# Layers of local attention: outputs by features, scores and outputs in one group each

## The chip, the cores and the metric

The kernel runs on one core of a Trainium2 chip. A core has five engines that run their own instruction queues in order and wait for one another through semaphores: TensorE (PE in the profile, with its weight loads as PEld), VectorE (DVE), ScalarE (ACT), GpSimd (POOL) and SyncE (SP, which here only issues DMAs). TensorE writes its results to PSUM; all other data of the kernel lies in SBUF. The metric is the device time of one launch in microseconds, the median of several runs.

## The reference

`x` holds 2 x 1024 tokens of 128 numbers. The network adds eight stages to it, one after the other. Six of them are small. Two are large and alike (`_L1_ffn_ref`, before and after the stage `L1_attn_b`): six layers, each made of local attention with 16 heads of 64 and a feed-forward block. Shortened:

```python
for i in range(6):
    x = attn_layer(shift_tokens(x), Wqkv[i], q_scale[i], k_scale[i], Wo[i]) + x
    x = ffn_layer(shift_tokens(x), ...) + x

def attn_layer(x, Wqkv, qs, ksc, Wo):        # x: b, 1024, 128
    q, k, v = split(x @ Wqkv)                # 16 heads of 64 each
    q, k = l2norm(q) * qs, l2norm(k) * ksc   # per head
    q, k = rotary(q), rotary(k)
    # windows of 32 queries see the 32 keys before them and their own 32
    attn = softmax(q . k * 8, masked)        # 32 x 64 per window and head
    return (attn @ v) @ Wo
```

`shift_tokens` takes the second half of the features from the token before. The feed-forward block is a layernorm, two products of 341 columns (one through an exact GELU), their product, and a product back to 128.

## The kernel before

The class `Layers` computes one such pass of six layers. Its unit is a tile of 128 tokens, `m`, numbered over layers, batches and tiles (`place`): 6 x 2 x 8 = 96 tiles per pass, 192 in both. All is in fp32. A tile takes these stages, named as methods:

- `project` (L1448): q and k, each in two halves of the rotary pair, four matmuls of 128 x 512 into PSUM banks of the pool `pj`. `squares` (L1457, ScalarE) writes the squares of a bank to SBUF, `rotate` (L1477, VectorE, two multiplications per bank) multiplies the same bank with rotary tables. The two engines read one PSUM bank one after the other, in the order in which the program names them.
- `halves`, `join`, `scale` (L1483, L1494, L1509, GpSimd): the sum of the halves' squares, the sum of the rotated parts, and the multiplication with the inverse length, which `lengths` (VectorE) and `inverses` (ScalarE: Relu, Ln, Exp) make.
- `flip` and `heads`: q and k transposed on TensorE (through the helper `to_psum`, whose transposes have line L201) and copied to SBUF by ScalarE.
- `project_v`, `values`, `windows`: v, copied to SBUF, and cut by DMAs on SP into `vw`, which holds for every window its 64 rows of v.
- `scores`: eight masks and 64 small matmuls per tile, in two parts of 32. A fp32 matmul is two instructions in the profile, each with its weight load.
- `below_max`, `exps`, `sums`: the softmax without its division; `sums` also makes the reciprocals `inv`.
- `flip_p`, `probabilities`: the exponentials transposed, so that keys lie on partitions, and copied to SBUF.
- `outputs` (L1647): 64 small matmuls in two parts. A block of transposed probabilities (64 keys x 32 queries) is loaded into the array and v (64 keys x 64 features) streams; the result has queries on partitions. `divide` (L1655, VectorE) multiplies with `inv` from PSUM to SBUF; `flip_o` transposes the result on TensorE (8 transposes); `features` (L1672, ScalarE) copies it to `outT`, with features on partitions.
- `project_out`, `add_out`: the product with `Wo`, and the addition to x.
- The feed-forward block works on four tiles at once (`ffn_...`, `gate...`, `value...`), so in one turn of four.

`turns` writes the order of all work by hand. The text `ORDER` lists stage names with arguments and a number: in turn n, the stage works on tile n minus that number, so a larger number is later and a negative one earlier. Each turn walks through the whole list, and every engine takes its instructions in that order; nothing is rescheduled. The numbers run from -3 to 11. `features` and `project_out` of a tile thus run two turns after its scores, and its `ffn_add` up to eleven turns after.

PSUM has eight banks: four in `pj` (projections, v, outputs, `y` and everything of the feed-forward block, handed out in turn), two for transposes (`tp`), two for scores. A piece of work that wants a bank waits for the last reader of the one that was handed out four (or two) before.

ScalarE's functions come in table sets. `gate` ends with an explicit load of the set that has Ln and Exp, when its three parts are done; the GELU's set is loaded when the first part runs. A load is inserted wherever a function is not in the set that is active.

## Time and profile before

| what | before |
|---|---|
| runs, us | 3993.75 median, 3986.62 to 4009.88 (3 runs) |
| span of the profiled execution, us | 3987.0 |
| TensorE busy | 3825.6 us, 96% |
| VectorE busy | 3116.1 us, 78% |
| GpSimd busy | 2535.5 us, 64% |
| ScalarE busy | 2414.0 us, 61% |
| granted TensorE clock, mean | 0.970 |

The profiled execution is one run; of its time the profile has the span from its first to its last instruction. Busy time is what the records of an engine cover; a matmul's record is longer than the time it keeps TensorE from the next (they are pipelined), so costs on TensorE are better read from the starts of successive work. A group line has the source line, the engine, the operation, tiles written and read, shapes, the count, the busy time of the group, the mean duration of one in ns, and the idle time before it with what ended it. A wait line names the waiting engine and line, what it waited for, and then the sum in us, the number of times and the longest. A windows line has, after the window's bounds and length, the busy us of each engine with instruction counts, the granted clock of TensorE, and the DMA engines' share. A timeline line has the start in us, the duration of the run of like instructions in us, and their count.

### The profile page before, as it was taken

How to read it: one execution, taken by the hardware profiler on the slowest of the kernel's cores; microseconds unless marked ns; L12 is line 12 of the kernel's file. 1: busy time of each engine (PE TensorE's matmuls, PEld its weight loads, DVE VectorE, ACT ScalarE, POOL GpSimd, SP SyncE). 2: the span in 40 equal slices, each digit the busy share in tenths (PEclk: the TensorE clock that was granted, in tenths of full speed). 3: DMA queues.
4: the chain of work that ended last, by engine and by line, in shares of the span. 5: the costliest groups of instructions: out<-in, count | busy, mean ns of one | idle time of the engine just before them, and what ended most of it. 6: DMA issues, size and time to landing. Idle time of an engine off the chain costs nothing.

```text
span 3987.0 us, 156275 instructions
## 1 busy us (share of the span) xinstructions
PE 3825.6 (96%) x67372; PEld 2521.5 (63%) x67372; DVE 3116.1 (78%) x6012; ACT 2414.0 (61%) x4582; POOL 2535.5 (64%) x1638
## 2 busy tenths in 40 slices
PE   7898979999999999999999779999999999999998
PEld 5646436666666666666666446666666666666665
DVE  7775877778787878787887667887878787878786
ACT  3444437766666666666666458666666666666665
POOL 4541448776766667767675467766767767666662
PEclk8899979999999999999999779999999999999999
DMA  3030313232333333323222033333333323332222
GB/s 87 2 85 8 79 62 75 67 92 69 78 84 75 78 78 73 88 72 77 63 70 67 9 95 70 75 85 75 86 71 73 92 68 77 85 76 67 66 68 54
DMA packets 217397, 281.11 MB, mean 71 GB/s; under 512 B 52493, under 2 KB 108682, under 8 KB 216586
## 3 DMA queue, kind: packets, MB, share of 16 engines
q1 hardware_dynamic: 216714, 271.12, 27.9%
q8 instruction: 536, 8.78, 1.0%
q14 instruction: 147, 1.20, 0.1%
HBM read 69.46 MB, written 3.28 MB: 18 GB/s over the span
## 4 chain that ended last, share of the span: by engine, by line
PE 87%; DVE 6%; DMA 2%; POOL 2%; ACT 1%; issue 1%; SPq 0%; DVEq 0%; POOLq 0%; ACTq 0%
PE pj_l L1448 17%; PE y_l L1679 9%; PE pv_l L1550 9%; PE tqk_l L201 9%; PE av_l L1647 8%; PE sc_l L1597 7%; PE tpr_l L201 4%; PE to_l L201 4%; PE fg_l L1753 3%; PE fy_l L1789 3%; PE fa_l L1774 3%; PE sc_l L1588 2%; DMA f0share_e<-f0d_e 1%; PE f0S_e L1239 1%; DVE t_l L1477 1%
## 5 line engine op out<-in xcount | busy, mean ns | idle before, releaser
L1477 DVE TENSOR_TENSOR t_l<-pj_l,rot_l 128x512 f32<-128x512 f32 x1536 | 968.1, 684 | 368.6 <-ACT sq_l L1457 356.6
L1494 POOL TENSOR_TENSOR raw_l<-t_l,t_l 128x1024 f32<-128x1024 f32 x384 | 907.8, 2364 | 532.5 <-DVE on_l L1655 285.0
L1448 PE MATMUL pj_l<-wqkv_l,x_l 128*128 128x512 f32 x1536 | 785.9, 614 | 6.5 <-DVE t_l L1477 4.2
L1509 POOL TENSOR_TENSOR raw_l<-raw_l,rn_l 128x1024 f32<-128x1024 f32 x384 | 723.2, 1902 | 94.6 <-ACT rn_l L1504 87.4
L1483 POOL TENSOR_TENSOR sq_l<-sq_l 128x512 f32<-128x512 f32 x384 | 490.8, 1278 | 311.8 <-ACT sq_l L1457 308.7
L1457 ACT ACTIVATE sq_l<-pj_l 128x512 f32<-128x512 f32 x768 | 461.5, 603 | 369.6 <-PE pj_l L1448 367.6
L201 PE MATMUL tqk_l<-ident_sb,raw_l 128*128 128x128 f32 x3072 | 452.7, 278 | 15.5 <-POOL raw_l L1509 13.9
L1527 ACT COPY qT_l<-tqk_l 128x512 f32<-128x512 f32 x384 | 224.8, 585 | 387.9 <-PE tqk_l L201 387.8
L201 PEld LDWEIGHTS tqk_l<-ident_sb,raw_l 128*128 128x128 f32 x3072 | 356.4, 142 | 160.7 <-issue 121.3
L1550 PE MATMUL pv_l<-wqkv_l,x_l 128*128 128x512 f32 x768 | 416.4, 624 | 6.1 <-DVE ln_xn_fl L1733 5.3
L1679 PE MATMUL y_l<-outT_l,wo_l 128*128 128x128 f32 x3072 | 393.7, 281 | 0.0
L1597 PEld LDWEIGHTS sc_l<-kT_l,qT_l 64*32 64x32 f32 x24576 | 295.4, 105 | 155.5 <-issue 145.1
L1679 PEld LDWEIGHTS y_l<-outT_l,wo_l 128*128 128x128 f32 x3072 | 357.5, 191 | 18.3 <-issue 1.0
L1448 PEld LDWEIGHTS pj_l<-wqkv_l,x_l 128*128 128x128 f32 x1536 | 256.3, 192 | 172.1 <-issue 111.2
L1647 PE MATMUL av_l<-vw_l,pT_l 64*32 64x64 f32 x24576 | 360.5, 224 | 2.1 <-issue 1.7
L1559 ACT COPY v_l<-pv_l 128x512 f32<-128x512 f32 x384 | 225.1, 586 | 225.4 <-PE pv_l L1550 205.5
L1655 DVE TENSOR_TENSOR on_l<-av_l,inv_l 128x512 f32<-128x512 f32 x384 | 247.4, 686 | 121.5 <-PE av_l L1647 121.3
L1647 PEld LDWEIGHTS av_l<-vw_l,pT_l 64*32 64x32 f32 x24576 | 294.2, 105 | 70.0 <-issue 63.6
L1597 PE MATMUL sc_l<-kT_l,qT_l 64*32 64x64 f32 x24576 | 329.8, 223 | 0.3 <-issue 0.3
L201 PEld LDWEIGHTS tpr_l<-ident_sb,pr_l 128*128 128x128 f32 x1536 | 189.1, 141 | 152.3 <-issue 116.8
L1607 DVE TENSOR_TENSOR pr_l<-sc_l,mx_l 128x512 f32<-128x512 f32 x384 | 265.6, 692 | 13.2
L201 PEld LDWEIGHTS to_l<-ident_sb,on_l 128*128 128x128 f32 x1536 | 183.2, 141 | 128.4 <-issue 110.9
(317 smaller groups left out, 6208.9 us busy)
## 6 DMA issues: line engine op xcount, KB each, us to landing
vw_l<-v_l SPq DMA_DIRECT2D x3024, 64.0 KB
wqkv_l<-in_Wqkv SPq DMA_DIRECT2D x36, 512.0 KB
f0share_e<-f0d_e SPq DMA_DIRECT2D x64, 256.0 KB
rot_l<-in_rotary SPq DMA_DIRECT2D x24, 512.0 KB
wo_l<-in_Wo SPq DMA_DIRECT2D x12, 512.0 KB
w_l<-in_W SPq DMA_DIRECT2D x12, 341.0 KB
a0rows<-a0both SPq DMA_DIRECT2D x4, 512.0 KB
a0qk<-a0rows SPq DMA_DIRECT2D x32, 64.0 KB
```

The costliest lines, as they stand in the source:

```text
L201: self.nc.tensor.transpose(tp[:, c, :], src(c), self.ident)
L1448: self.nc.tensor.matmul(pj.rearrange("p h d -> p (h d)"), self.x[b][0][:, ts(a, P)], self.w[i]["qkv"][:, ds(INNER * s + 512 * u, 512)], st ...
L1457: self.nc.scalar.activation(st["sq", s][:, u], st["pj", s, u], AF.Square)
L1477: self.nc.vector.tensor_tensor(to, st["pj", s, u], tabs[:, k, None, ts(w, LD // 2)].to_broadcast(half), ALU.mult)
L1483: self.nc.gpsimd.tensor_tensor(sq[:, 0], sq[:, 0], sq[:, 1], ALU.add)
L1494: self.nc.gpsimd.tensor_tensor(r.rearrange("p h u d -> p u h d"), st["t1", s], st["t2", s], ALU.add)
L1509: self.nc.gpsimd.tensor_tensor(r, r, st["rn"][:, ts(s, LH), None].to_broadcast([P, LH, LD]), ALU.mult)
L1550: self.nc.tensor.matmul(pj, self.x[b][0][:, ts(a, P)], self.w[i]["qkv"][:, ds(2 * INNER + 512 * r, 512)], start=True, stop=True,)
L1597: nc.tensor.matmul(sc[j][ts(c, 32), hp, :], st["q"][rows, hp, ts(c, 32)], st["k"][rows, hp, ds(32 * c, 64)], start=False, stop=(hp == 7),)
L1607: nc.vector.tensor_tensor(p, st["sc"][j], mx[:, :, None].to_broadcast([P, 8, 64]), ALU.subtract)
L1647: nc.tensor.matmul(av[r][ts(c, 32), q, j, :], st["pT", j][rows, q, ts(c, 32)], st["vw"][rows, c, ts(2 * q + j, LD)], start=True, stop=True,)
L1679: self.nc.tensor.matmul(y[:, 0:P], self.w[i]["o"][:, c, :], st["o"][:, c, :], start=(c == 0), stop=(c == 7))
```

## The change

1. `outputs` is turned over: v (64 keys x 64 features) is loaded into the array and the transposed probabilities (64 keys x 32 queries) stream, so that the result has features on partitions. Its 64 matmuls are one group.
2. `flip_o` is gone; `features` copies from the outputs' banks.
3. `divide` now works on the exponentials in SBUF, in place, before `flip_p`.
4. `scores` is one group.
5. `ORDER` is another one. The numbers run from -3 to 12: all projections are three turns early, outputs two turns late (one before), the parts of the GELU lie in three turns (9, 10 and 11; before all in 9), `ffn_add` is at 12. In one of the four projections the rotation is named before the squares, in the other three after; before, the squares came first in all four.

```diff
 ORDER = """
-    value_in1:11 halves0:-2 join0:-2 add_out:3 flip11:0 divide0:2 divide1:2 project_v0:0 ffn_flip:7
-    heads01:0 flip_p0:1 gate_in0:9 heads11:0 value_in0:11 lengths1:-1 value1:11 value_in2:10 values0:0
-    scores0:0 lengths0:-2 inverses:-1 project10:-2 ffn_back:8 flip_p1:1 ffn_stats:7 gate0:9 value0:11
-    ffn_out:11 ffn_dev:7 squares10:-2 sums:1 ffn_norm:7 project11:-2 carry:0 project00:-3 value2:10
-    rotate10:-2 scores1:0 probabilities0:1 squares11:-2 project_v1:0 ffn_gain:8 probabilities1:1
-    flip_o0:2 scale1:-1 ffn_add:11 gate_in2:9 flip_o1:2 windows0:0 rotate11:-2 squares00:-3 values1:0
-    scale0:-1 gate_in1:9 rotate00:-3 features0:2 features1:2 below_max0:0 halves1:-2 gate2:9
-    below_max1:0 project01:-3 flip10:-1 gate1:9 squares01:-3 exps0:0 outputs0:1 join1:-2 heads10:-1
-    rotate01:-3 project_out:2 flip00:-1 heads00:-1 exps1:0 outputs1:1 flip01:-1 windows1:0
+    lengths0:-2 divide0:1 ffn_gain:9 flip_p1:1 project00:-3 gate2:10 ffn_dev:8 ffn_norm:8 gate1:11
+    probabilities1:1 squares00:-3 scores:0 scale0:-1 values0:0 value2:11 lengths1:-2 outputs:2
+    features0:2 scale1:-1 join1:-2 flip_p0:1 flip00:-1 probabilities0:1 ffn_add:12 rotate00:-3
+    project01:-3 features1:2 value_in0:11 project_v1:0 windows0:0 below_max1:0 below_max0:0
+    project10:-3 squares01:-3 rotate01:-3 exps1:0 exps0:0 halves0:-3 values1:0 value0:11 heads00:-1
+    flip10:-1 value_in1:11 rotate10:-3 windows1:0 sums:0 carry:0 value1:11 heads10:-1 squares10:-3
+    project_out:3 divide1:0 project11:-3 flip01:-1 add_out:3 ffn_flip:7 gate_in0:9 gate_in1:10
+    squares11:-3 flip11:-1 join0:-3 ffn_back:8 heads01:-1 gate_in2:9 ffn_stats:7 value_in2:10
+    inverses:-2 project_v0:-1 heads11:-1 gate0:9 rotate11:-3 ffn_out:11 halves1:-3
 """
...
-    def scores(self, m, part):
+    def scores(self, m):
...
-        for hp in range(4 * part, 4 * part + 4):
+        for hp in range(8):
...
-        inv = st["inv"] = self.small.tile([P, 2, 4, 2], F32, tag="inv", name=f"inv_{key}")
-        nc.vector.reciprocal(inv, sm.rearrange("p j (q r) -> p r q j", r=2))
+        inv = st["inv"] = self.small.tile([P, 2, 8], F32, tag="inv", name=f"inv_{key}")
+        nc.vector.reciprocal(inv, sm)
+
+    def divide(self, m, j):
+        p = self.get(m)["p", j]
+        self.nc.vector.tensor_tensor(
+            p, p, self.get(m)["inv"][:, j, :, None].to_broadcast([P, 8, 64]), ALU.mult
+        )
...
-    def outputs(self, m, part):
+    def outputs(self, m):
         nc, st, key = self.nc, self.get(m), self.name(m)
-        if part == 0:
-            st["av"] = [self.pj.tile([P, 4, 2, LD], F32, tag="pj", name=f"av_{key}_{r}") for r in range(2)]
-        av = st["av"]
-        for q in range(2 * part, 2 * part + 2):
-            for j in range(2):
-                for c in range(4):
+        av = st["av"] = [self.pj.tile([P, 4, P], F32, tag="pj", name=f"av_{key}_{r}") for r in range(2)]
+        for q in range(4):
+            for c in range(4):
+                for j in range(2):
                     for r in range(2):
                         rows = slice(64 * r, 64 * r + 64)
                         nc.tensor.matmul(
-                            av[r][ts(c, 32), q, j, :], st["pT", j][rows, q, ts(c, 32)],
-                            st["vw"][rows, c, ts(2 * q + j, LD)], start=True, stop=True,
+                            av[r][ts(j, LD), q, ts(c, 32)], st["vw"][rows, c, ts(2 * q + j, LD)],
+                            st["pT", j][rows, q, ts(c, 32)], start=True, stop=True,
                         )
-
-    def divide(self, m, r):
-        st = self.get(m)
-        on = st["on", r] = self.sp.tile([P, 4, 2, LD], F32, tag="on", name=f"on_{self.name(m)}_{r}")
-        self.nc.vector.tensor_tensor(
-            on, st["av"][r], st["inv"][:, r, :, :, None].to_broadcast([P, 4, 2, LD]), ALU.mult
-        )
-
-    def flip_o(self, m, r):
...
-        self.nc.scalar.copy(st["o"].rearrange("p (q r) t -> p r q t", r=2)[:, r], st["to", r])
+        self.nc.scalar.copy(st["o"].rearrange("p (q r) t -> p r q t", r=2)[:, r], st["av"][r])
```

## The prediction

> **What bounds the kernel now.** I read the stage windows first, then what VectorE waits for in the same stretch, then the groups that the diff touches, then the timeline for prices that the two passes of `Layers` do not show.
>
> ```profile
> core 0: us, PE busy (x) PEld busy (x) DVE busy (x) ACT busy (x) POOL busy (x), PEclk, DMA share, GB/s
> 800.00:1200.00 400.00, 399.85 (x7848) 268.83 (x7847) 321.37 (x600) 256.04 (x498) 279.03 (x176) 1.00 0.33 81
> 2900.00:3300.00 400.00, 400.00 (x7858) 270.52 (x7857) 321.06 (x600) 256.21 (x500) 275.73 (x175) 1.00 0.32 76
> ```
>
> Inside both passes TensorE has no gap and its granted clock is 1.00. One turn of the loop gives VectorE 21 instructions, and every fourth turn 17 more for the feed-forward block, so 25.25 on average; 600 of them in 400 us are 23.75 turns of 16.84 us. I work in groups of four turns, 67.4 us; the two passes hold 192 turns, 48 groups. Of a group VectorE is busy 80.3%, 54.2 us; ScalarE 64%, 43.1; GpSimd 70%, 47.0. So TensorE sets the pace, and VectorE stands 13.2 us per group behind it.
>
> ```profile
> DVE t_l L1477 <- ACT sq_l L1457: 134.1, 97, 2.5
> DVE on_l L1655 <- PE av_l L1647: 46.5, 71, 1.1
> DVE x_l L1693 <- PE y_l L1679: 35.4, 53, 0.9
> DVE t_l L1477 <- POOL sq_l L1483: 3.4, 8, 0.4
> DVE x_l L1695 <- PE fy_l L1789: 2.8, 18, 0.2
> ```
>
> These are VectorE's waits from 800 to 2000 us (17.8 groups), 12.5 us per group. The longest is a rotation waiting for the squares of the same projection; the second is the division, waiting for TensorE.
>
> ```profile
> L201 PE MATMUL to_l<-ident_sb,on_l 128*128 128x128 f32 x1536 | 207.5, 273 | 1.0 <-ACT pT_l L1635 1.0
> L1655 DVE TENSOR_TENSOR on_l<-av_l,inv_l 128x512 f32<-128x512 f32 x384 | 247.4, 686 | 121.5 <-PE av_l L1647 121.3
> L1763 ACT ACT_TABLE_LOAD x48 | 61.6, 1283 | 0.8
> ...
> 2003.41 0.84 PE L1597 MATMUL sc_l<-kT_l,qT_l 64*32 64x64 f32 x64
> 2004.18 0.70 PE L1448 MATMUL pj_l<-wqkv_l,x_l 128*128 128x512 f32 x1
> ...
> 55.68 1.16 PE L1006 MATMUL a0av<-a0pT,a0v 128*8 128x64 f32 x64
> 202.26 0.95 PE L1129 MATMUL f0lg_e<-f_sb,f0x_e 128*128 128x8 f32 x8
> ...
> 2127.29 1.27 POOL L1483 TENSOR_TENSOR sq_l<-sq_l 128x512 f32<-128x512 f32 x1 [3.02 <-ACT sq_l L1457]
> 2127.32 1.78 DVE L1371 TENSOR_TENSOR xt<-xt,x_l 64x512 f32<-64x512 f32 x1
> ...
> 2190.31 0.69 DVE L1371 TENSOR_TENSOR xt<-xt,x_l 64x512 f32<-64x512 f32 x1
> ```
>
> The reader is to see three things. A half group of scores (64 instructions) takes 0.77 us from its start to the next work's start. A form with v held in the array exists already, in `attn_a0`. And an addition on VectorE with both inputs in SBUF takes 0.69 us with GpSimd idle, but 1.78 us when a GpSimd operation began 0.03 us before it: it ends 0.54 us after that operation's end. Other pairs (L1236, L1262, L1371) give 0.55.
>
> **The change, part by part.**
>
> *TensorE.* The transposes of the divided output go: 8 per turn, 0.107 us from start to start (four take 0.43 on the timeline), 0.87 us. Scores in one group: now two halves of 0.77 to 0.79, 1.58 by the upper. In the single records the first 32 instructions of a half start within 0.24 us, then 0.09 us pass, then they come 8.3 ns apart; the switch to small tiles and back is about 0.1 us before and 0.15 behind. One group of 128 is then 0.33 + 96 x 0.0083 + 0.15 = 1.27 us: 0.31 less, and 0.10 for one switch in. The bounds are nothing gained (1.58) and 1.0 (all at 6.7 ns).
>
> Outputs keep 128 instructions per turn, but each loads 64 columns and streams 32, on four array tiles, where it loaded 32 and streamed 64 on eight. No row has this. In the `f0lg` records 128 columns load every 112 ns, whatever streams behind, so 64 columns are 56 ns; `a0av`, also on four tiles, moves four instructions per 56 ns. By both, 14 ns each: 128 x 14 = 1.79, and 0.15 out, 1.94 against 1.74 now (13.4 ns each from start to start, by the records between 1000 and 2000 us), less 0.10 for one switch. The low bound is the scores' 1.27; the high one has load and stream in a row, 84 ns for four tiles, 21 ns each, 2.84. I take 1.94, since two rows agree on it. Per turn: -0.87 - 0.41 + 0.10 = -1.18; TensorE falls to 62.7 us per group. Alone that would be 4.7 x 48 = 226 us gained.
>
> *VectorE.* The two divisions stay two per turn and of the same size, but move: from PSUM onto the probabilities in SBUF, ahead of the transposes. They are the only operations of these passes with two SBUF inputs on VectorE, and meet GpSimd, which is 70% busy. Alone they cost what they cost now (0.69 against 686 ns), so the price is the wait: what is left of the GpSimd operation, less 0.14. The longest (`join`, L1494) is 2.36 us, so it lies between 0 and 2.2. By place: `divide0` stands one reduction (0.65 us) behind the last rotation, which releases `join1`; if GpSimd is free then, 2.36 - 0.65 - 0.14 = 1.57 are left; if a scale still runs, about 0.8. `divide1` stands 2.8 us behind the third rotation, which releases a join, a half-sum and two scales, 7.4 us without a gap; the mean rest of those (squares of 2.36, 1.28, 1.90, 1.90 over twice their sum) is 0.97, so 0.83. I take 1.15 for each: 8 x 1.15 = 9.2 us per group, and VectorE's own demand is 63.4. GpSimd's operation that starts meanwhile loses 0.3 to 0.5 (a half-sum at 2132.88 us took 1.73 instead of 1.28); 4 us on 47 stay hidden.
>
> The Trainium skill (SBUF — State Buffer, Who interferes with whom) says that a VectorE instruction with two SBUF inputs and a GpSimd one that reads SBUF exclude each other for a whole instruction. It speaks against this change; the pairs above agree in kind. By the rule as written the division would follow with its whole 0.69 us, 0.14 more each, and the total below would be 54 us higher.
>
> What queues behind: behind `divide0` the other length, the first rotation (its PSUM bank is wanted by a v projection) and TensorE's `flip_p0`; behind `divide1` the `add_out`, the last rotation, and `flip_p1`, now TensorE's first work of the next turn. Before, the transposes needed only the exponentials.
>
> The wait on outputs (46.5) goes with the old place. The squares wait (134.1, 7.5 per group) goes too: with all projections three turns ahead, and in the changed order one rotation of the four standing before its squares, a VectorE that is late finds the squares done. So the description holds for three of four pairs, as before, and not for the fourth. Waits for `y`, `fy` and the half-sums stay: 41.6 / 17.8 = 2.3 us per group.
>
> *ScalarE.* The copies change source, not size. But the three GELUs of a block, now in one turn, spread over three turns (`gate0:9`, `gate2:10`, `gate1:11`), and exponentials and logarithms come between the second and third. The order of the built instructions has four more table loads per group (before the exponentials, two in `inverses`, before the last GELU), 176 in all. At 1.283 us, 5.1 per group. ScalarE goes to 48.2 and is no bound on average, but that turn has 14.9 us of work. The two in `inverses` stand just before the last head copy, which the next scores wait for; there the cover is gone, and VectorE's maxima follow. The other two lie beside VectorE's late work. Bounds 0 and 5.1; I take 2.6, the two.
>
> *Fill.* `ffn_add` moves from 11 to 12 turns late, one more turn per pass that holds two additions of 0.75: 3 us. Outputs read the windows of v a turn later; those have two buffers, so the DMAs on SP wait for the outputs two tiles back, and later loads wait behind them. The windows are read two turns on, so I take nothing; if that cover went, the nearest row is the copy of v that waits for these DMAs today (L1559, 19.3 us over 85 waits, 0.23 each), 44 us if once a turn.
>
> **Sum.** VectorE 63.4 + waits that stay 2.3 + loads 2.6 = 68.3 us per group, against TensorE's 62.7 and 67.4 before. +0.9 x 48 = 43, and 3: 46 us. The profiled execution's span is 3987.0, so 4033; the runs' median 3993.75 is 6.75 above that span (start and end of the launch lie around it), so 4040 us.
>
> **Rivals.**
> *TensorE stays the bound.* It decides where a division waits less than (62.7 - 54.2 - 2.3) / 8 = 0.78 us with the loads hidden. For it: the engine is packed today over all VectorE's waits. Against: the rest of a running GpSimd operation. Time 3994 - 226 + 3 = 3771.
> *VectorE binds, the loads are hidden.* 65.7 per group: -82, 3915. For it: ScalarE has a third of its time free. Against: the 14.9 us turn.
> *Every division meets a join that has just begun*, 1.7 to 2.2 us each: 72.7 to 76.7 per group, 4250 to 4440. For it: joins are released by VectorE itself. Against: GpSimd, two scales behind, is seldom free then.
> *Outputs load and stream in a row*, 2.84: TensorE 66.3, hidden under 68.3 in the forecast; it would lift the first rival to 3945.
>
> **How the numbers follow.** Forecast 0.46 (own range 3985 to 4150), heavier stalls 0.16, TensorE bound 0.14, loads hidden 0.20, the last row moving times inside these. A measurement here tells 0.5% (20 us) from no change. Of the forecast's case about a quarter lies within it: same 0.11; slower 0.35 + 0.16 and 0.04 for late starts that I can't price, 0.55; faster 0.14 + 0.20 = 0.34. Range 3830 to 4240: it leaves out most of the first rival and the top of the third.
>
> **What would show it.** Right: TensorE under 96% with waits for `pr_l` at the first transposes of a turn; the division's mean near 1.8 us, its minimum 0.69; 176 more table loads; no `to_l`; outputs near 15 ns each from start to start. Wrong: a division's mean under 1.3 with a packed TensorE (first rival), or outputs above 20 ns.

## The result, and the profile after

The changed kernel takes 4260.1 us (median of 4 runs, 4238.8 to 4292.7) against 3995.8 us before (4 runs, 3986.6 to 4009.9). The ratio is 1.0665, with a 95% interval of 1.0613 to 1.0716: 265 us lost. The forecast was 4040, its range ended at 4240.

The profile's page of the changed kernel, its busy times and the share of its DMA queues (queue, kind: packets, MB, share of the DMA engines' time):

```profile
PE 3833.8 (90%) x65836; PEld 2629.9 (62%) x65836; DVE 3260.5 (77%) x6012; ACT 2609.7 (61%) x4758; POOL 2591.0 (61%) x1638
...
q8 instruction: 525, 8.60, 0.9%
```

The windows of the two passes, columns as in the prediction:

```profile
core 0: us, PE busy (x) PEld busy (x) DVE busy (x) ACT busy (x) POOL busy (x), PEclk, DMA share, GB/s
800.00:1200.00 400.00, 371.14 (x7100) 263.10 (x7099) 319.82 (x567) 257.69 (x482) 266.25 (x165) 0.97 0.30 74
2900.00:3300.00 400.00, 371.80 (x6829) 263.08 (x6829) 311.66 (x554) 254.82 (x473) 256.00 (x159) 0.94 0.29 70
```

TensorE is no longer packed (371 of 400 us), but VectorE is no busier than before (320 against 321): no engine is full now. TensorE's granted clock went from 1.00 to 0.97 and 0.94. What TensorE lacks shows in the groups of the changed kernel:

```profile
L1649 PE MATMUL av_l<-pT_l,vw_l 64*64 64x32 f32 x24576 | 559.3, 226 | 211.7 <-issue 170.0 <-ACT fh_l L1749 23.9 <-DVE ln_xn_fl L1719 9.7
...
L1623 DVE TENSOR_TENSOR pr_l<-pr_l,inv_l 128x512 f32<-128x512 f32 x384 | 404.7, 1054 | 5.2
...
L1595 PE MATMUL sc_l<-kT_l,qT_l 64*32 64x64 f32 x24576 | 288.5, 225 | 15.6 <-ACT kT_l L1527 14.7 <-issue 0.8
...
L1749 ACT ACT_TABLE_LOAD x92 | 118.0, 1283 | 1.6
```

The same line for the outputs of the kernel before:

```profile
L1647 PE MATMUL av_l<-vw_l,pT_l 64*32 64x64 f32 x24576 | 360.5, 224 | 2.1 <-issue 1.7
```

TensorE now stands idle inside the outputs for 211.7 us, where it stood idle for 2.1. Of this, 170.0 us are "issue": time in which it waited for nothing that the profile shows. From the starts of successive instructions, in the whole turns between 1000 and 2000 us (58 before, 54 after), in us per turn:

| | before | after |
|---|---|---|
| turn | 16.87 | 18.04 |
| outputs | 1.72 | 3.95 |
| scores (without masks) | 1.57 | 1.50 |
| transposes of the result | 0.87 | 0 |
| transposes of the probabilities | 0.90 | 1.11 |

All other rows move by 0.1 or less, most of them down. So within a turn the outputs make the loss: 2.2 us more, less 0.87 for the transposes that went. From the first to the last outputs of the two passes 212 of the 265 us are lost (1676 and 1696 us against 1579 and 1580). 31 us lie ahead of the first outputs of the passes, which now come a turn later (75.2 and 75.6 us behind the first projection, before 58.8 and 61.2), 18 us between the passes. One turn, TensorE's timeline in the changed kernel (start, duration, operation, count, idle before):

```profile
1210.11 1.02 PE L1448 MATMUL pj_l<-wqkv_l,x_l 128*128 128x512 f32 x2
1211.07 0.41 PE L1587 MATMUL sc_l<-wide_l,identb_l 64*32 64x512 bf16 x8
1211.29 1.46 PE L1595 MATMUL sc_l<-kT_l,qT_l 64*32 64x64 f32 x128
1212.68 1.21 PE L1649 MATMUL av_l<-pT_l,vw_l 64*64 64x32 f32 x41
1214.89 1.48 PE L1649 MATMUL av_l<-pT_l,vw_l 64*64 64x32 f32 x87 [1.00 <-issue]
1216.30 0.66 PE L201 MATMUL tpr_l<-ident_sb,pr_l 128*128 128x128 f32 x4
```

The group stops after 41 of its 128 instructions. No other engine releases it. The trace also records the packets of the queue that brings instructions to the core. Those near this turn, from start to landing in us:

```
1202.03 1203.46
1212.53 1213.65
1216.04 1216.96
```

A packet lands at 1213.65 and TensorE goes on at 1214.89, 1.24 us later. That is the rule: of the 192 groups of outputs 141 have a gap over 0.6 us in the middle (195.9 us in sum), and for nine in ten of them the gap ends 1.22 to 1.56 us after a packet has landed. Each packet has 16,384 bytes. TensorE has 131,672 matmuls and weight loads; over the 525 packets of q8 that is 251 for each, and 256 with its 2784 semaphore instructions (which do nothing but handle a semaphore).

The order of TensorE's instructions shows that these gaps belong to the packets. The matmul at which the group stops differs from turn to turn, from the 10th to the 127th of its 128. But if all of TensorE's instructions ahead of the point where it goes on are counted (matmuls, loads and semaphore instructions), the count leaves 193 or 194 when divided by 256, for each of the 141 gaps. So every gap stands at the same place of a packet of 256. A wait for another engine would belong to a certain instruction of the group instead.

The scores with their masks (136 products) and the outputs (128) are 264 products with as many loads, 528 instructions or 2.1 packets, in one row. At their own pace they would use up a packet in 1.7 us; packets of one hurried pair start 3.5 us apart (here 1212.53 and 1216.04; in the passes 95% of all distances are above 3.45). The kernel before has at most 72 such products (half of the scores with the masks), 144 instructions, before something long comes.

What waits in the meantime, from the changed kernel's waits between 800 and 2000 us:

```profile
ACT outT_l L1658 <- PE av_l L1649: 225.8, 58, 7.4
...
DVE t_l L1477 <- ACT sq_l L1457: 133.7, 77, 4.0
...
PE av_l L1649 <- issue: 63.1, 56, 3.1
```

ScalarE stands before the copies of the outputs, 3.9 us in most turns, and the rotations wait for the squares as much as before (134.1).

The clock falls behind the gaps. One of them, with TensorE's windows around it (columns as above) and a line of its timeline:

```profile
core 0: us, PE busy (x) PEld busy (x) DVE busy (x) ACT busy (x) POOL busy (x), PEclk, DMA share, GB/s
1179.52:1182.93 3.41, 1.14 (x74) 1.14 (x73) 2.79 (x5) 0.00 (x0) 0.35 (x1) 1.00 0.24 94
1182.93:1186.34 3.41, 3.41 (x19) 2.48 (x12) 0.69 (x1) 1.66 (x3) 0.51 (x1) 0.50 0.29 69
1186.34:1189.75 3.41, 3.41 (x20) 2.32 (x19) 2.49 (x5) 3.08 (x6) 2.20 (x3) 1.00 0.30 70
...
1181.79 1.30 PE L1649 MATMUL av_l<-pT_l,vw_l 64*64 64x32 f32 x74 [3.10 <-issue]
```

In the two passes the granted clock falls to one half in 56 stretches of 3.4 or 6.8 us, 229 us in all (in the kernel before, one stretch of 3.4 us). In them an instruction of a projection takes 853 ns from start to start, otherwise 431. In the 3.4 us directly ahead of each stretch, TensorE ran no matmul for 22% of the time or more (median 39%), and ahead of 47 of the 56 one of the 141 gaps reaches into them. Of the gaps over 2 us, 15 of 16 were followed by a stretch within 3.4 us, of those under 1 us 1 of 39. The clock is not the cause of the gaps: 127 of the 141 end at the full clock. But it makes them dearer; at half the pace, by at most half of the 229 us (an estimate).

The first theory, "place" or "supply", was: **TensorE runs out of instructions in the row of scores and outputs.** The rivals: the new form of the outputs is slow by itself ("form"); the gaps are a wait for another engine that the profile doesn't show ("dependencies"; the count above speaks against it); VectorE or ScalarE set the pace, as the prediction had it.

The Trainium skill (Runtime: NRT & Kernel Launch, Instruction fetch mechanics) says that instructions are refilled in blocks of 16 KiB, 256 instructions, that the next block is fetched while the current one runs, and that this is mostly hidden. The size agrees with the 16,384 bytes here. That it is hidden holds for the kernel before (one such gap in all its outputs, 1.1 us) and fails here.

### The profile page after: what moved, and what is told of

Read it like the earlier page. It is cut to its first block, busy times and chain, and to the rows that moved or that the text cites. A ratio compares the mean times of both kernels' runs of the same rounds, so it can differ in the third digit from the quotient of the medians.

```text
span 4252.3 us, 153395 instructions
## 1 busy us (share of the span) xinstructions
PE 3833.8 (90%) x65836; PEld 2629.9 (62%) x65836; DVE 3260.5 (77%) x6012; ACT 2609.7 (61%) x4758; POOL 2591.0 (61%) x1638
## 4 chain that ended last, share of the span: by engine, by line
PE 56%; DVE 18%; ACT 14%; issue 7%; POOL 3%; DMA 2%; SPq 0%; ACTq 0%; DVEq 0%; POOLq 0%
PE av_l L1649 11%; PE pj_l L1448 11%; PE tqk_l L201 5%; PE y_l L1665 5%; PE pv_l L1550 4%; DVE t_l L1477 4%; PE tpr_l L201 4%; PE sc_l L1595 3%; DVE pr_l L1623 3%; ACT sq_l L1457 2%; PE fg_l L1739 2%; ACT L1503 2%; ACT L1504 1%; ACT L1749 1%; PE fa_l L1760 1%
## 5 line engine op out<-in xcount | busy, mean ns | idle before, releaser
L1448 PE MATMUL pj_l<-wqkv_l,x_l 128*128 128x512 f32 x1536 | 832.1, 626 | 13.6 <-DVE t_l L1477 8.0
L1483 POOL TENSOR_TENSOR sq_l<-sq_l 128x512 f32<-128x512 f32 x384 | 528.9, 1377 | 419.6 <-ACT sq_l L1457 419.3
L1649 PE MATMUL av_l<-pT_l,vw_l 64*64 64x32 f32 x24576 | 559.3, 226 | 211.7 <-issue 170.0
L1649 PEld LDWEIGHTS av_l<-pT_l,vw_l 64*64 64x64 f32 x24576 | 512.2, 140 | 254.5 <-issue 186.5
L1658 ACT COPY outT_l<-av_l 128x512 f32<-128x512 f32 x384 | 226.2, 589 | 624.8 <-PE av_l L1649 624.5
L1623 DVE TENSOR_TENSOR pr_l<-pr_l,inv_l 128x512 f32<-128x512 f32 x384 | 404.7, 1054 | 5.2
L1489 DVE TENSOR_REDUCE ss_l<-sq_l 128x16 f32<-128x512 f32 x384 | 259.2, 676 | 84.2 <-POOL sq_l L1483 83.0
L1639 ACT COPY pT_l<-tpr_l 128x512 f32<-128x512 f32 x384 | 224.3, 584 | 127.9 <-PE tpr_l L201 124.6
L1595 PE MATMUL sc_l<-kT_l,qT_l 64*32 64x64 f32 x24576 | 288.5, 225 | 15.6 <-ACT kT_l L1527 14.7
L201 PE MATMUL tpr_l<-ident_sb,pr_l 128*128 128x128 f32 x1536 | 264.0, 298 | 25.0 <-DVE pr_l L1623 14.5
```

The source lines that it names most:

```text
L201: self.nc.tensor.transpose(tp[:, c, :], src(c), self.ident)
L1448: self.nc.tensor.matmul(pj.rearrange("p h d -> p (h d)"), self.x[b][0][:, ts(a, P)], self.w[i]["qkv"][:, ds(INNER * s + 512 * u, 512)], st ...
L1483: self.nc.gpsimd.tensor_tensor(sq[:, 0], sq[:, 0], sq[:, 1], ALU.add)
L1595: nc.tensor.matmul(sc[j][ts(c, 32), hp, :], st["q"][rows, hp, ts(c, 32)], st["k"][rows, hp, ds(32 * c, 64)], start=False, stop=(hp == 7),)
L1623: self.nc.vector.tensor_tensor(p, p, self.get(m)["inv"][:, j, :, None].to_broadcast([P, 8, 64]), ALU.mult)
L1649: nc.tensor.matmul(av[r][ts(j, LD), q, ts(c, 32)], st["vw"][rows, c, ts(2 * q + j, LD)], st["pT", j][rows, q, ts(c, 32)], start=True, stop ...
```

## The experiments

All ratios are to the kernel before, measured beside it on the same chip; the changed kernel stands at 1.0665. "Gaps" are those over 0.6 us inside the outputs, without the one behind the second instruction, which is a wait for a PSUM bank.

### Is it VectorE or ScalarE? (e12, e7)

```diff
-    lengths0:-2 divide0:1 ffn_gain:9 flip_p1:1 project00:-3
+    lengths0:-2 ffn_gain:9 flip_p1:1 project00:-3
...
-    project_out:3 divide1:0 project11:-3
+    project_out:3 project11:-3
```

> The changed kernel without its two divisions per turn; the probabilities stay undivided. It takes 405 us of VectorE's work away (384 x 1.054 us). The prediction had VectorE at the limit; then it gives back at least the divisions' own 2.1 us per turn down to TensorE's demand, 4252 - 350 = 3900. Theory 'supply': VectorE is not the limit, and only the waits of the first transposes for the division go (14.5 us) with some of the rotations' lateness: 4180 to 4250.

Measured: 4267.3 us, 1.0672 (1.0641 to 1.0704), the changed kernel's ratio. Windows of this run:

```profile
core 0: us, PE busy (x) PEld busy (x) DVE busy (x) ACT busy (x) POOL busy (x), PEclk, DMA share, GB/s
800.00:1200.00 400.00, 370.40 (x7109) 263.14 (x7108) 273.69 (x521) 258.72 (x483) 257.44 (x163) 0.97 0.30 74
```

VectorE lost 46 us of work in 400 and nothing became faster; the gaps stayed (145, 219 us). VectorE does not set the pace, and the divisions' wait for GpSimd shows no cost here.

```diff
-    lengths0:-2 divide0:1 ffn_gain:9 flip_p1:1 project00:-3 gate2:10 ffn_dev:8 ffn_norm:8 gate1:11
+    lengths0:-2 divide0:1 ffn_gain:9 flip_p1:1 project00:-3 ffn_dev:8 ffn_norm:8
...
-    ffn_flip:7 gate_in0:9 gate_in1:10
+    ffn_flip:7 gate_in0:9 gate_in1:9
...
-    heads11:-1 gate0:9 rotate11:-3
+    heads11:-1 gate0:9 gate1:9 gate2:9 rotate11:-3
```

> The changed kernel with the three parts of the GELU again in one turn, one behind the other, and the second gate product moved into that turn: 176 table loads fewer, 226 us of ScalarE's work. The prediction put half of it on the path (2.6 us per block of four tiles, 125 us): 4120 to 4150. If TensorE's instruction supply is the bound, ScalarE's loads lie beside it and the time is 4220 to 4270; the wait of the outputs for a bank that a GELU still holds (0.75 us in every fourth turn, 36 us) may go, which makes 4215 to 4235.

Measured: 4293.3 us, 1.0746 (1.0709 to 1.0784): not faster, rather a little slower. ScalarE's work fell from 258 to 230 us in the window, the 176 loads are gone, and the idle time in the outputs grew:

```profile
L1649 PE MATMUL av_l<-pT_l,vw_l 64*64 64x32 f32 x24576 | 552.2, 226 | 222.3 <-issue 202.4 <-DVE ln_xn_fl L1719 8.8 <-ACT v_l L1559 7.0
```

The wait for the GELU's bank (23.9 us) went as expected, "issue" rose by 32 us, and 280 us of the passes ran at half clock (229 in the changed kernel). No cost of the loads shows.

### Is it the form? (e1, e11)

The kernel before with only the outputs turned over:

```diff
-            for j in range(2):
-                for c in range(4):
+            for c in range(4):
+                for j in range(2):
...
-                            av[r][ts(c, 32), q, j, :], st["pT", j][rows, q, ts(c, 32)],
-                            st["vw"][rows, c, ts(2 * q + j, LD)], start=True, stop=True,
+                            av[r][ts(j, LD), q, ts(c, 32)], st["vw"][rows, c, ts(2 * q + j, LD)],
+                            st["pT", j][rows, q, ts(c, 32)], start=True, stop=True,
...
-    flip_o0:2 scale1:-1 ffn_add:11 gate_in2:9 flip_o1:2 windows0:0
+    scale1:-1 ffn_add:11 gate_in2:9 windows0:0
```

> The kernel before with one part of the change: its order, its two halves of scores and of outputs and its division (PSUM to SBUF, behind the outputs) stay; only the outputs are turned over (v loaded, probabilities streamed) and the eight transposes of the result are left out. The division still multiplies the same block with the same reciprocals, which now meet the wrong tokens, so its work is kept and its meaning is not. Theory 'place' (the 30.9 ns per outputs instruction of the changed kernel come from where the group stands: behind 128 scores, where eight semaphore instructions, 125 ns apart, and a gap of 0.8 to 3 us that ends 1.4 us after an instruction packet has landed are not covered): outputs near 15 ns each, 1.8 to 2.1 us per turn against 1.74, TensorE's demand falls by 0.87 - 0.3 = about 0.6 us per turn, 192 turns: 3995 - 115, so 3850 to 3930. Theory 'form' (64-column loads are slow wherever they stand): outputs above 25 ns each, over 3.2 us per turn, and 3995 + 192 x (1.5 - 0.87) = 4110 or more.

Measured: 3953.7 us, 0.9893 (0.9872 to 0.9913). Its outputs:

```profile
L1647 PE MATMUL av_l<-pT_l,vw_l 64*64 64x32 f32 x24576 | 481.8, 221 | 7.2 <-issue 5.7 <-ACT pT_l L1635 1.4
```

Four gaps in all. A half group takes 1.066 us where no semaphore instruction stands in it, 14.6 ns for each instruction and 0.13 us to change over; with the halves that hold them, outputs take 2.33 us per turn. So the form costs 0.61 us per turn against 1.72, the transposes give 0.87, and the 1.1% gained, 43 us, are 0.22 per turn, against a difference of 0.26. The time is 24 us above what was expected of "place", since the outputs are a little dearer than the 2.1 us allowed for; "form" wanted 4110.

The opposite, the old form in the new place:

```diff
-                            av[r][ts(j, LD), q, ts(c, 32)], st["vw"][rows, c, ts(2 * q + j, LD)],
-                            st["pT", j][rows, q, ts(c, 32)], start=True, stop=True,
+                            av[r][ts(c, 32), q, ts(j, LD)], st["pT", j][rows, q, ts(c, 32)],
+                            st["vw"][rows, c, ts(2 * q + j, LD)], start=True, stop=True,
```

> The changed kernel with the outputs in the old form (probabilities loaded, 32 columns, v streams, 64 columns), in the new place and in one group; the result has tokens on partitions and is copied as if it had features, so every output stands in the wrong place, and all else is as in the changed kernel. By itself an instruction takes 13.4 ns in place of 14.6 to 16.6. Theory 'supply': the number of instructions sets the time of scores and outputs, so the form hardly matters here: 4200 to 4270, outputs above 3.4 us per turn, gaps over 0.6 us as many as before or more. Theory 'form': outputs fall under 2.4 us per turn, 3950 to 4100.

Measured: 4174.4 us, 1.0442 (1.0402 to 1.0482); outputs 3.71 us per turn, 147 gaps of 216 us. The form is worth 86 us in this place, more than "supply" allowed for (4200 at least). Part of it can be the clock, at half for 120 us of the passes and not 229; why it fell less is open. But the gaps do not go with the form, and outputs that took 1.72 us in the kernel before take 3.71 here.

### Is it the row? (e9, e10, e6, e4)

The same useless product, once between the scores and the outputs (e9), once far away (e10):

```diff
+        self.nc.tensor.matmul(
+            av[0].rearrange("p q t -> p (q t)"), self.w[self.place(m)[0]]["qkv"][:, 0:P],
+            self.w[self.place(m)[0]]["qkv"][:, 0:512], start=True, stop=True,
+        )
```

> The changed kernel with useless work put between the scores and the outputs: one product of 128 x 512 with its own weights, 0.86 us of TensorE per turn (two instructions), into the bank that the outputs then overwrite. 192 x 0.86 = 165 us if TensorE's time is what counts there. Theory 'supply': the gap that follows an instruction packet shrinks by what the product takes, so it is nearly free: the gaps inside the outputs fall from 1.0 us per turn to 0.2 to 0.4, the time stays at 4240 to 4310. If the gaps are something else, they stay and the time goes to 4370 to 4430.

> The same useless product in another place of the changed kernel: ahead of the last projection of k, into that projection's bank, far from the scores and the outputs. Theory 'supply': here nothing shrinks to make room for it, and it costs most of its 165 us less what TensorE waits elsewhere: 4360 to 4430. If it is as free as between scores and outputs, TensorE does not set the pace at all and the gaps are beside the point: 4240 to 4300.

Measured: between them, 4213.4 us, 1.0558 (1.0512 to 1.0605); far away, 4401.8 us, 1.1012 (1.0976 to 1.1047). Outputs with the product between:

```profile
L1653 PE MATMUL av_l<-pT_l,vw_l 64*64 64x32 f32 x24576 | 476.1, 222 | 96.3 <-issue 90.0 <-ACT v_l L1559 4.9
```

and with the product far away:

```profile
L1654 PE MATMUL av_l<-pT_l,vw_l 64*64 64x32 f32 x24576 | 561.2, 226 | 222.6 <-issue 184.6 <-ACT fh_l L1754 20.3 <-DVE ln_xn_fl L1724 9.5
```

These two runs decide whether the place matters. 165 us of work put into the row make the kernel 1% faster than without it (47 us by the medians); the same work elsewhere costs 142 us. The gaps fell to 82 of 98 us in the first and stayed at 151 of 215 us in the second. The half clock went with them: 72 us of the passes in e9, 225 us in e10. These two runs alone do not exclude a hidden wait for another engine, which a pause of 0.86 us at the right place could shorten too. The count of instructions does: in e9 and e10, and in every other kernel below that has scores and outputs in one group each, all these gaps end at a remainder of 193 to 195. The difference of place, 47 + 142 = 189 us, is an estimate of what the row costs at least, its effect on the clock included, of the 265 us lost.

Half as many instructions in the outputs:

```diff
-            for c in range(4):
+            for c in range(2):
...
-                            av[r][ts(j, LD), q, ts(c, 32)], st["vw"][rows, c, ts(2 * q + j, LD)],
-                            st["pT", j][rows, q, ts(c, 32)], start=True, stop=True,
+                            av[r][ts(j, LD), q, ts(c, 64)], st["vw"][rows, 2 * c + q % 2, ts(2 * q + j, LD)],
+                            st["pT", j][rows, q, ts(c, 64)], start=True, stop=True,
```

> The changed kernel with half as many instructions in the outputs: the probabilities of two windows (64 columns) stream over the v of one of them, 64 instructions instead of 128. It leaves out the v of every second window, so half the outputs are formed with the wrong window; what is written and copied keeps its size. By the 14.6 ns of an instruction alone this saves 64 x 14.6 ns = 0.93 us per turn, 180 us: 4070 to 4100 at best. Theory 'supply' expects more than that, since the gap goes with the length of the row: outputs 3.95 to 1.3 to 1.8 us per turn, fewer than 30 gaps over 0.6 us, and a time that the other engines set, 3900 to 4030.

Measured: 3980.9 us, 0.9959 (0.9942 to 0.9976): 279 us less than the changed kernel, where the instructions' own time is 180 us. The other 99 us lie in the gaps, which fell by as much, and in the half clock, which fell from 229 to 48 us of the passes. The time is as expected. But the outputs took 2.38 us, not 1.3 to 1.8, and 70 gaps of 97 us stayed: 200 products in a row are still too many.

The semaphore instructions ahead of the products that wait for the windows' DMAs, eight per turn and 125 ns apart, moved away by reading the windows early:

```diff
+        if (s, u) == (1, 1) and m >= 4:
+            old = self.get(m - 4)
+            for c in range(4):
+                for r in range(2):
+                    rows = slice(64 * r, 64 * r + 64)
+                    self.nc.tensor.matmul(
+                        flat[ts(r, 64), ts(c, 32)], old["vw"][rows, c, ts(r, LD)],
+                        old["pT", 0][rows, 0, ts(c, 32)], start=True, stop=True,
+                    )
```

> The changed kernel with 16 more small TensorE instructions per turn (8 matmuls of the outputs' own form) that read the windows of v a turn ahead, ahead of the last projection of k and behind the eight matmuls with Wo, into the bank that this projection then overwrites. They take the semaphore instructions for the windows' DMAs away from the outputs to a place with 0.9 us of long work ahead of it. Price: 16 x 15 ns and a switch of 0.25 us, about 0.4 to 0.5 us per turn. Theory 'place': outputs lose about 0.8 us per turn (3.95 to 3.1), net 0.3 to 0.4 us x 192 gained: 4170 to 4220; the gaps that follow instruction packets stay. If the semaphore instructions cost nothing by themselves, the additional work makes it 4300 to 4350.

Measured: 4327.2 us, 1.0826 (1.0785 to 1.0868). The semaphore instructions are gone from the outputs, but these hardly gained (3.84 us), because the gaps grew from 196 to 256 us: what came earlier waited for the same packet. The additional 0.59 us per turn (112 us) were paid in part, 67 us. The gain that "place" expected was missed; the time is that of the other case, 4300 to 4350: the semaphore instructions had cost little by themselves, since the packet set the end.

### Can the row be taken apart? (e2, e5, e13, e16)

Four kernels moved useful work in between. The outputs later:

```diff
-    probabilities1:1 squares00:-3 scores:0 scale0:-1 values0:0 value2:11 lengths1:-2 outputs:2
-    features0:2 scale1:-1 join1:-2 flip_p0:1 flip00:-1 probabilities0:1 ffn_add:12 rotate00:-3
-    project01:-3 features1:2 value_in0:11
+    probabilities1:1 squares00:-3 scores:0 scale0:-1 values0:0 value2:11 lengths1:-2
+    scale1:-1 join1:-2 flip_p0:1 flip00:-1 probabilities0:1 ffn_add:12 rotate00:-3
+    project01:-3 outputs:2 features0:2 features1:2
+    value_in0:11
```

> The changed kernel, with the outputs (and the copies of their result) moved in the written order from directly behind the scores to behind the second projection of q: two groups of four transposes and one projection, 1.8 us of long TensorE instructions, now stand between the two groups of 128 small ones. Theory 'place': both the semaphore instructions and the instruction supply get cover, outputs fall from 3.95 us per turn to 2.0 to 2.3, the gaps over 0.6 us inside the group from 141 to fewer than 30, and up to 1.7 us per turn is gained until VectorE's work (about 15 us per turn with its stalls) comes through: 3930 to 4060. Theory 'form': outputs stay above 3.5 us per turn, 4230 to 4290.

The first projection between them:

```diff
-    flip_p1:1 project00:-3 gate2:10
+    flip_p1:1 scores:0 project00:-3 gate2:10
...
-    squares00:-3 scores:0 scale0:-1
+    squares00:-3 scale0:-1
```

> The changed kernel with one word of its order moved: the first projection of q (0.93 us in two long instructions) stands between the scores and the outputs instead of ahead of the scores. Everything behind the outputs keeps its place, which the run with the outputs moved away did not allow (there the transposes came 2.3 us earlier and waited for their inputs). Theory 'supply' (TensorE runs out of instructions in a row of 264 small matmuls with 264 loads, and goes on 1.4 us after the next packet has landed): the packet gets 0.93 us more, so the gaps inside the outputs shrink by up to that much; outputs 3.95 to about 3.0 to 3.3 us per turn, 4252 - 0.7 x 192 = about 4120, 4070 to 4190. Theory 'dependencies' (the gaps are a wait for another engine's work and merely coincide with packets): no gain, 4230 to 4310, and the gaps stay as many and as long.

The second projection between them:

```diff
-    lengths1:-2 outputs:2
+    lengths1:-2 project01:-3 outputs:2
...
-    project01:-3 features1:2 value_in0:11
+    features1:2 value_in0:11
```

> The changed kernel with the second projection of q (0.86 us) moved three places ahead, between the scores and the outputs; the two groups of transposes that stood ahead of it now follow the outputs. It takes the place of the useless product of the run before, so no work is added and nothing that needs other engines comes earlier. Theory 'supply': the gaps shrink as with the useless product (from about 1.2 to 0.7 us per turn), and its 0.86 us are not paid: 4213 - 165 x (0.5 to 1) = 4050 to 4130. If the next limit (waits for the other engines) stands close behind, as where the first projection was moved, 4180 to 4240.

The outputs at the head of the turn:

```diff
-    lengths0:-2 divide0:1 ffn_gain:9
+    outputs:2 lengths0:-2 divide0:1 ffn_gain:9
...
-    lengths1:-2 outputs:2
+    lengths1:-2
```

> The changed kernel with its outputs at the head of the turn, ahead of the first transposes and the first projection of q; 1.4 us of long TensorE work then stand between them and the scores. Their inputs are there since the turn before. Theory 'supply': the gaps over 0.6 us in outputs and scores together fall to less than half (196 us to under 90), and, if no bank holds the outputs up, 4050 to 4150. If the outputs wait for the bank that the last addition or rotation of the turn before still reads, the gain is eaten up: 4200 to 4280.

| kernel | us | ratio | gaps, us | "issue" in the outputs, us |
|---|---|---|---|---|
| changed | 4260.1 | 1.0665 | 141, 196 | 170.0 |
| e2, outputs later | 4325.6 | 1.0827 | 43, 68 | 58.9 |
| e5, first projection between | 4240.2 | 1.0616 | 58, 78 | 70.8 |
| e13, second projection between | 4295.1 | 1.0751 | 70, 87 | 102.8 |
| e16, outputs first | 4526.0 | 1.1314 | 19, 27 | 45.6 |

In each the gaps shrank to half or less, as the supply theory says, and in each the time that it gave was missed, because another wait took their place. The 4240 us of e5 are what "dependencies" gave, but that asked for gaps as many and as long. A fifth order, e3, with the outputs in two parts of 64 instructions and the second behind the first projection of v, ends in a deadlock, so it has no time. In e16 the outputs wait for banks that a GELU and the normalisation still read, and 533 us of the passes run at half clock:

```profile
L1649 PE MATMUL av_l<-pT_l,vw_l 64*64 64x32 f32 x24576 | 631.8, 246 | 346.3 <-ACT fh_l L1749 180.7 <-DVE ln_xn_fl L1719 119.5 <-issue 45.6
```

In e5 it is the addition of the feed-forward block:

```profile
L1649 PE MATMUL av_l<-pT_l,vw_l 64*64 64x32 f32 x24576 | 535.5, 229 | 154.1 <-DVE x_l L1681 72.3 <-issue 70.8 <-DVE ln_xn_fl L1719 5.1
```

In e13 it is a bank with a copy of v (70.5 us). In e2 the transposes came early and waited for the copy that frees their bank, and for the division (TensorE's waits from 800 to 2000 us):

```profile
PE tqk_l L201 <- ACT pT_l L1640: 38.9, 16, 2.5
PE tpr_l L201 <- DVE pr_l L1624: 21.9, 23, 1.5
```

So the useless product did what none of these could: it filled the row and moved nothing else in the order. How much a new order for the whole turn would win back was not tried.

### What are the other parts worth? (e15, e8, e14, e17)

The scores in one group, in the kernel before:

```diff
-    scores0:0 lengths0:-2
+    scores:0 lengths0:-2
...
-    rotate10:-2 scores1:0 probabilities0:1
+    rotate10:-2 probabilities0:1
```

> The kernel before with one part of the change: the scores in one group, at the place of the first half. The prediction gave this 0.41 us of TensorE's time per turn with the switch (0.31 in the group, 0.10 for the switch): 3996 - 79 = 3915 to 3930 if TensorE stays packed. By the changed kernel's rows (1.50 us per turn against 1.57) it gives 0.07 and perhaps a switch, 13 to 30 us: 3965 to 3985. If 136 small products in a row already outrun the supply, or the longer group makes others late, 4000 or more.

Measured: 4000.9 us, 1.0013 (0.9997 to 1.0029): nothing. The scores take 1.66 us per turn where two halves took 1.57:

```profile
L1645 PE MATMUL av_l<-vw_l,pT_l 64*32 64x64 f32 x24576 | 365.4, 224 | 11.6 <-issue 10.5 <-DMA vw_l<-v_l 0.3
...
L1595 PE MATMUL sc_l<-kT_l,qT_l 64*32 64x64 f32 x24576 | 313.0, 225 | 17.6 <-issue 16.9
```

In 2650 us of the two passes (700 to 2000 and 2500 to 3850), 40 steps of over 0.3 us from one small matmul to the next end 1.15 to 1.6 us behind a packet (35 us); in the kernel before 7 do (4 us). The outputs, in halves as before, rose too, from 1.72 to 1.85 us per turn, and of the 0.22 us per turn that the two rows lost the projections gave back 0.16 (5.46 to 5.30 us). Of the rows tried here, 72 products do not stall and 136, 272 instructions and so a little over one packet, begin to.

The turned-over outputs, complete, with the changed kernel's division in SBUF, in the order of before (halves of scores and outputs as there):

```diff
-    flip11:0 divide0:2 divide1:2 project_v0:0
+    flip11:0 project_v0:0
...
-    heads01:0 flip_p0:1 gate_in0:9 heads11:0 value_in0:11
+    heads01:0 gate_in0:9 heads11:0 features0:2 features1:2 value_in0:11
...
-    sums:1 ffn_norm:7
+    sums:1 divide0:1 divide1:1 ffn_norm:7
...
-    flip_o0:2 scale1:-1 ffn_add:11 gate_in2:9 flip_o1:2 windows0:0
+    flip_p0:1 scale1:-1 probabilities0:1 ffn_add:11 gate_in2:9 flip_p1:1 probabilities1:1 windows0:0
...
-    scale0:-1 gate_in1:9 rotate00:-3 features0:2 features1:2 below_max0:0
+    scale0:-1 gate_in1:9 rotate00:-3 below_max0:0
```

> The turned-over outputs, with the division on the exponentials in SBUF, complete and in the order of before: scores and outputs stay in two halves each, far apart, the transposes of the probabilities move to where the transposes of the result were, the copies of the result to where the divisions were. If all that the changed kernel loses comes from its order (scores and outputs in one row, GELU parts spread), this is as fast as the form alone: TensorE without a gap, outputs 2.3 us per turn, 3910 to 3990, below the kernel before. If the division's move into SBUF (a wait for GpSimd each time) or its place ahead of the transposes costs what the prediction said (1.15 us for each), VectorE sets the pace: 4040 or more.

Then with ScalarE's sequence changed:

```diff
-    flip_p0:1 scale1:-1 probabilities0:1 ffn_add:11 gate_in2:9 flip_p1:1 probabilities1:1 windows0:0 rotate11:-2 squares00:-3 values1:0
+    flip_p0:1 scale1:-1 ffn_add:11 gate_in2:9 flip_p1:1 squares00:-3 probabilities0:1 windows0:0 rotate11:-2 values1:0
+    probabilities1:1
```

> The first complete kernel with the turned-over outputs in the order of before, with two changes to ScalarE's sequence: the squares of the first projection of q stand ahead of the copy of the first transposed probabilities, and the copy of v between the two copies. In the first attempt ScalarE waited 2.7 us in almost every turn at that copy, with those squares, a rotation and a bank behind it. If that was what took away the 1.1% that the form alone gains, this comes to 3920 to 4020, at or below the kernel before. If the division's place ahead of the transposes is what costs (the transposes wait for sums, reciprocal and division of the same turn), it stays above 4150.

And with the normalisation ahead of the divisions:

```diff
-    sums:1 divide0:1 divide1:1 ffn_norm:7
+    sums:1 ffn_norm:7 divide0:1 divide1:1
```

> The complete turned-over outputs in the order of before, with the normalisation of the block moved ahead of the two divisions on VectorE. In the run before, a projection waited for it for 2.6 us per block, 48 blocks, 123 us: 4168 - 123 = 4045, 4020 to 4110. To reach the kernel before (3997) the waits of the transposes' copies for sums and division would have to go too; below 4000 would mean that the form pays for itself.

Measured: 4268.9 us, 1.0683 (1.0655 to 1.0711); 4167.7 us, 1.0425 (1.0408 to 1.0443); 4077.6 us, 1.0202 (1.0173 to 1.0231). The first is as slow as the changed kernel with none of its gaps: in this order other waits set the pace. Each of the two that were removed gave back 90 to 100 us, less than hoped for in the first case (4168 for 3920 to 4020) and as expected in the second. None of the three has the gaps (1, 4 and 3). Windows and division of the last:

```profile
core 0: us, PE busy (x) PEld busy (x) DVE busy (x) ACT busy (x) POOL busy (x), PEclk, DMA share, GB/s
800.00:1200.00 400.00, 393.71 (x7572) 268.66 (x7571) 343.31 (x582) 250.52 (x492) 287.26 (x173) 0.99 0.33 80
```

```profile
L1655 DVE TENSOR_TENSOR pr_l<-pr_l,inv_l 128x512 f32<-128x512 f32 x384 | 452.2, 1216 | 5.0
```

TensorE is at 98% again and VectorE at 86%. Of the complete kernels in the new form it came nearest to the kernel before, but it stays 2% behind, and 124 us behind e1, which has the same outputs and divides from PSUM. What differs from e1 is the division and the order that it asks for. How much of the 124 us is its wait for GpSimd (0.53 us for each by the means, 1.216 against 0.686) and how much its place ahead of the transposes is open. No complete kernel here beats the one before.

## Why the prediction was wrong

Slower was the likelier side (0.55), but for a reason that fell: that the sign was right is luck. The time lies 20 us above the range.

- **The term that failed: the outputs, 1.94 us per turn.** Measured 3.95; the high bound of 2.84 was too low as well. The pace of an instruction was right (14.0 ns worked out from two rows, 14.6 measured in e1), and at that pace the group needs 128 x 14.6 ns and 0.13 us, 2.0 us (2.33 in e1, with the semaphore instructions, which the sum left out). What was missing is that a group has its own pace only while instructions arrive. The prediction timed the two groups one by one, took 0.10 us off for the switch saved, and let them stand in one row at no charge. Its test, "outputs above 20 ns", pointed at the right row: 30.9 ns. That the clock falls behind the gaps, 229 us at one half, was not foreseen either. (The 1.74 us for the old outputs are 128 x 13.4 ns = 1.72; this changes nothing.)
- **Scores in one group, 0.41 us saved:** not found. 1.50 us per turn in the changed kernel (predicted 1.27), and no gain at all in e15.
- **The transposes, 0.87 us saved:** right; the row is gone, and e1 has the gain, less the dearer outputs.
- **VectorE as the bound (63.4 us per group, with 1.15 us of wait at each division):** wrong twice. The mean wait is 1.054 - 0.686 = 0.37 us, inside the bounds of 0 and 2.2 but a third of the value taken; the sum over the rests of GpSimd's operations assumed it busy at every division, and the median division, 0.692 us, met no wait. And e12 shows that VectorE is not on the path. That two SBUF inputs meet GpSimd at all (the Trainium skill, SBUF — State Buffer, Who interferes with whom) is right: the minimum is 0.659 us, the longest 2.75.
- **176 more table loads at 1.283 us:** right in number, wrong in price. Of 5.1 us per group, 2.6 were put on the path; e7 gives none back.
- **The rotations' wait for the squares would go:** it stayed, 133.7 us from 800 to 2000 us in place of 134.1.
- **Fill, 3 us:** about 31. It counted the turn more as two additions; ahead of the first outputs of each pass it took 16.4 and 14.4 us.
- **Rivals.** "Every division meets a join", 4250 to 4440, holds the measured time, and is refuted all the same by the mean of 0.37 us and by e12. "Outputs load and stream in a row" named the right group with a wrong mechanism: e1 has the same loads at 14.6 ns.

## What to carry to other kernels

Before small products are merged into longer groups or moved next to each other, count the instructions (a fp32 product is two matmuls and two loads) against what the instruction queue delivers: here one packet of about 250 per 3.5 us, so that a row of 270 began to stall and one of 528 lost 1 us per turn on average, and more through the clock. Long instructions between small ones can then be no loss but the time in which the next packet arrives, as in e9; in e2, e5, e13 and e16 the move brought other waits. "Issue" as the cause of idle time inside a group on TensorE is the place in the profile to look for it. The count of the engine's instructions at the ends of the gaps tells from one trace whether they belong to the packets, and a piece of useless work put there and, as a control, elsewhere tells in two runs what the place costs.

## What was not expected of the hardware

- The instruction queue can bound TensorE: packets of 16,384 bytes took 0.9 to 1.4 us, hardly ever started less than 3.3 us apart, and TensorE went on about 1.4 us after one had landed.
- Adding 0.86 us of work per turn made a kernel faster by 1% (e9).
- A semaphore instruction of TensorE takes 125 ns to the next; about eight of them inside a group cost little more where a packet sets the end (e4).
- Short stops can halve TensorE's granted clock for the next 3.4 us or more: 56 times in the two passes of the changed kernel, behind 15 of the 16 gaps over 2 us and 1 of the 39 under 1 us.
- Merging two groups of small products into a row longer than a packet gained nothing (e15).
